# Cross attention on one NeuronCore: scores in row quarters of the array, values in column halves

## The chip, the cores and the metric

The kernel runs on one core of one Trainium2 chip. The metric is the device time of one execution in microseconds (us), as the median of several runs. Beside it stands one execution that the hardware profiler recorded; its trace is what all readings of instructions come from.

## The reference

Two batches of 1024 tokens with 256 features pass four residual blocks in fp32. Only the first is touched by the change: cross attention of the tokens to 77 context rows, with 16 heads of 16 features and a mask on the context rows.

```python
Q = split_heads(query @ Wq.T + bq)     # query: layernorm(x), 2 x 1024 x 256
K = split_heads(key @ Wk.T + bk)       # key, value: the context, 2 x 77 x 256
V = split_heads(value @ Wv.T + bv)
scores = jnp.einsum('bhqd,bhkd->bhqk', Q, K) / scale
scores = jnp.where(mask == 0, -1e10, scores)
attn = jax.nn.softmax(scores, axis=-1)
h = jnp.einsum('bhqk,bhkd->bhqd', attn, V)
return h @ Wo.T + bo
...
x = x + cross_attention(layernorm(x), context)
x = x + self_attention_on_4_of_16_heads(layernorm(x))
x = x + gelu(layernorm(x) @ context.T) @ context      # per batch
x = x + top1_mixture_of_8_experts(layernorm(x))
```

The second block picks four heads per batch from a mean over all tokens, so its weights can be read from memory only when the last tile of that batch has left the first block.

## The kernel before

The 2048 tokens are 16 tiles of 128 (one token a partition). Stage A is the cross attention, one tile after the other, in a software pipeline: `a_step(s)` (L506) issues the scores of tile s, the transposes of the weights of tile s−1, the values of tile s−2, the transpose of the heads' outputs of s−3 and the output projection of s−4. Stage B (self attention, context block and the router) and the experts follow.

**Order.** The whole body stands under a manual schedule for TensorE (PE), VectorE (DVE), ScalarE (ACT) and GpSimd (POOL): each of these engines executes its instructions in the order of the program text. Further work is hung into the steps by a plan: `at("a", s, pos, f, ...)` places f in step s at position pos, and `take` calls what is due. In stage A these are mainly `query` (projection of 512 tokens of the queries, at steps 2, 5, 6, 8 and 9), `do_turn` (transposes of the normalized rows `y_a` and `y_b`, written to `lps`, at steps 1, 3, 4, 5, 7 and, for the second block, 6, 8, 10, 12, 14), `do_rows` (layernorm), and for the second block `route_sums`, `route_mean`, `route_logits`, `route_heads` (step 14: choice of heads and reads of their weights) and `b_qk`. Reads from memory are issued by SyncE, three of them by ScalarE.

**Scores** (`a_scores`, L421). The 256 features are two column groups m of 128, which are 8 heads each. For a column group, a tile's queries stand transposed in `qTa` (features by tokens). The keys stand in `kblk` in block form: for one of HG = 4 heads j a copy of all keys that `hmask` has set to zero outside that head's 16 features and scaled. So a product over 64 partitions, half of the array's rows, gives the scores of 4 heads with 4 × 77 = 308 columns. The two halves gg of the rows write to the two banks of one PSUM tile `sc`. A second product in bf16 (L439) adds −1e10 where the mask is zero: `ones16` times `mneg`, in which three rows of each half hold the three bf16 parts of the number. An fp32 product is two passes, each with a weight load of its own, so one tile has 8 + 4 matmuls.

**Weights of the attention** (`a_weights`, L449). Per column group: DVE takes the maximum per head (`mx`, L453) and subtracts it (`e`, L455), ACT takes the exponential (L459). The two PSUM tiles of a step are the two buffers of the pool `big`.

**Transposes** (`a_transposed`, L461). The 16 × 77 = 1232 weights of a token are cut into 10 chunks of 128; PE transposes them in blocks of 4, 4 and 2 chunks into `pt`, ACT copies each block to `eT` (L469). `pt`, `hps`, `lps` and the other transposes take the two buffers of the pool `trp` (tag `tr`) in turn.

**Values** (`a_values`, L471). Per chunk one product of all 128 tokens with `vblk`: the rows of three heads, masked, and a column of ones for the sum of the weights (3 × 17 = 51 columns), added up in the PSUM tile `av`. After it, in the same function, DVE takes the reciprocal of the sums (`rc`) and normalizes (`hn`). `av`, `po_a`, `qps`, `kps` and others take the two buffers of `accp` (tag `acc`) in turn.

**Start** (L1432 on). In the order of the text: transposes of Wq (`turn_weight`), layernorm of tiles 0 to 3, statistics of tiles 4 to 7 (`do_rows`), transposes of the context (`cps`), of Wk, of the first normalized rows (`do_turn`), key projections `context_k(0)` and `(1)` with the bias `bk_c` and the masked copies to `kblk`, query projections, transposes of Wv, and then the steps. The biases of queries and keys, `bq_c` and `bk_c`, are read as columns by `col_load` (L144): one element for each partition and column group.

## Time and profile before

| | us |
|---|---|
| runs | 623.37, 622.35, 623.32; median 623.32 |
| profiled execution | 623.49 |
| its span, first to last instruction | 621.8 |
| PE busy in the span | 581.7 |
| PE weight loads | 429.3 |
| DVE busy | 359.9 |
| ACT busy | 234.7 |
| POOL busy | 162.0 |
| first scores of tile 0 | at 18.08 |
| first scores of tile 15 | at 121.81 |

Busy times can lie beside each other: the engines work at the same time, and weight loads (PEld) beside the products. Matmuls are pipelined and their ends in the trace are modelled, so the time that a series of them takes is read from one start to the next, not from the sum of durations. In an order in time, each row has the start and length, the engine, the line, the operation, what it writes and reads, the shapes and the number of instructions merged; a bracket tells how long the engine had been idle, and for whom it waited. The granted TensorE clock is 0.978 of full speed in the mean, and full in the first 160 us.

### The profile page before, as it was taken

What the parts mean: (1) busy time and instruction counts of PE and PEld (TensorE: products, weight loads), DVE (VectorE), ACT (ScalarE), POOL (GpSimd) and SP (SyncE); (2) the same over time, 40 slices, a digit from 0 to 9 for tenths busy, and PEclk for the clock granted to TensorE, in tenths of its full rate; (3) what the DMA queues carried; (4) which work ended last, traced back from release to release, by engine and by line L of the source; (5) the groups of instructions that cost most, each with busy time, mean ns of one, the idle gap of its engine ahead of it and who ended that gap; (6) DMA issues with size and microseconds to landing.
All of it is one profiled execution on the core that took longest, in us unless ns stands there. A gap on an engine that the chain in (4) does not pass through costs nothing. (4 is left out here: it accounts for less than half of the span.)

```text
span 621.8 us, 10102 instructions
## 1 busy us (share of the span) xinstructions
PE 581.7 (94%) x3722; PEld 429.3 (69%) x3722; DVE 359.9 (58%) x939; ACT 234.7 (38%) x476; POOL 162.0 (26%) x204
## 2 busy tenths in 40 slices
PE   5999999989999999999999999996797999999994
PEld 4578878866655556656555656564596999999994
DVE  6767667852874356658665767676546433333331
ACT  3555545542655355445445555440021012111110
POOL 6656233222200020403021222200401233333321
PEclk9999999999999999999999999997689899999998
DMA  7100000020001000001000100011993799999940
GB/s 233 34 2 2 1 0 2 1 61 1 1 19 41 1 1 18 17 1 36 1 34 1 35 2 34 2 35 72 353 338 119 255 362 323 360 372 371 344 144 11
DMA packets 49674, 62.75 MB, mean 101 GB/s; under 512 B 11513, under 2 KB 42708, under 8 KB 49622
## 3 DMA queue, kind: packets, MB, share of 16 engines
q1 hardware_dynamic: 46352, 54.04, 25.8%
q0 software_dynamic: 2560, 7.34, 3.2%
q8 instruction: 31, 0.51, 0.3%
q10 hardware_dynamic: 709, 0.68, 0.3%
q14 instruction: 22, 0.17, 0.1%
HBM read 55.76 MB, written 6.82 MB: 101 GB/s over the span
## 5 line engine op out<-in xcount | busy, mean ns | idle before, releaser
L716 DVE TENSOR_REDUCE bnm<-bsc 128x1 f32<-128x1024 f32 x64 | 75.2, 1216 | 14.9 <-PE bsc L702 14.9
L1131 PE MATMUL ph<-ybT,w1s 128*128 128x128 f32 x640 | 79.7, 284 | 3.9 <-DVE ybT L1116 3.9
L1131 PEld LDWEIGHTS ph<-ybT,w1s 128*128 128x128 f32 x640 | 78.4, 200 | 6.0 <-DVE ybT L1116 5.1
L728 PE MATMUL bpt<-ident,be 128*128 128x128 f32 x512 | 73.1, 280 | 3.2 <-DVE v L678 1.2
L1150 PE MATMUL epo<-w2s,ehT 128*128 128x256 f32 x320 | 75.6, 380 | 0.0
L728 PEld LDWEIGHTS bpt<-ident,be 128*128 128x128 f32 x512 | 55.6, 140 | 27.9 <-issue 10.1
L718 ACT ACTIVATE be<-bsc,bnm 128x1024 f32<-128x1024 f32 x64 | 70.8, 1113 | 8.3 <-DVE bnm L716 7.9
L729 DVE COPY beT<-bpt 128x512 f32<-128x512 f32 x64 | 43.9, 686 | 50.4 <-PE bpt L728 50.4
L1138 ACT ACTIVATE ehT<-ph,b1s 128x128 f32<-128x128 f32 x80 | 22.9, 369 | 116.3 <-PE ph L1131 115.1
L702 PE MATMUL bsc<-kT,qT 64*128 64x512 f32 x256 | 64.6, 615 | 0.0
L738 PE MATMUL bov<-beT,v 128*64 128x256 f32 x512 | 63.4, 391 | 0.0
L1150 PEld LDWEIGHTS epo<-w2s,ehT 128*128 128x128 f32 x320 | 57.9, 190 | 6.3
L729 ACT COPY beT<-bpt 128x512 f32<-128x512 f32 x64 | 37.5, 586 | 62.4 <-PE bpt L728 61.4
L1140 DVE TENSOR_SCALAR ehT<-ph,b1s 128x128 f32<-128x128 f32 x80 | 22.5, 343 | 61.2 <-ACT ehT L1138 56.8
L738 PEld LDWEIGHTS bov<-beT,v 128*64 128x64 f32 x512 | 34.4, 139 | 24.6 <-issue 9.4
L1162 POOL DMA_INDIRECT out_dram<-ob,etok x20 | 20.5, 1023 | 94.2 <-DMA out_dram<-ob,etok 40.5
L750 POOL COPY brb<-brc 128x256 f32<-128x256 f32 x16 | 6.4, 398 | 146.5 <-DVE brc L748 146.5
L702 PEld LDWEIGHTS bsc<-kT,qT 64*128 64x128 f32 x256 | 22.5, 186 | 25.1 <-issue 20.7
L477 PE MATMUL av<-vblk,eT 128*128 128x51 f32 x320 | 37.4, 272 | 0.8 <-DVE hn L485 0.8
L477 PEld LDWEIGHTS av<-vblk,eT 128*128 128x128 f32 x320 | 37.1, 192 | 1.6 <-DVE hn L485 1.1
L453 DVE TENSOR_REDUCE mx<-sc 128x8 f32<-128x616 f32 x32 | 25.3, 792 | 16.6 <-PE sc L439 16.6
L469 ACT COPY eT<-pt 128x512 f32<-128x512 f32 (+1 forms) x48 | 23.0, 515 | 25.9 <-PE pt L468 25.1
(253 smaller groups left out, 854.2 us busy)
## 6 DMA issues: line engine op xcount, KB each, us to landing
w1s<-in_L_ffn_w_dram SPq DMA_DIRECT2D x20, 1024.0 KB
w2s<-in_L_ffn_w_dram SPq DMA_DIRECT2D x20, 1024.0 KB
b2s<-in_L_ffn_b_dram SPq DMA_DIRECT2D x20, 128.0 KB
xs<-in_x_dram SPq DMA_DIRECT2D x4, 512.0 KB
ztok<-xs SPq DMA_DIRECT2D x16, 128.0 KB
ztok<-y_d SPq DMA_DIRECT2D x16, 128.0 KB
ws_k<-in_L_ffn_Wk_dram SPq DMA_DIRECT2D x8, 64.0 KB
ws_q<-in_L_ffn_Wq_dram SPq DMA_DIRECT2D x8, 64.0 KB
```

The source lines that it names most:

```text
L453: nc.vector.tensor_reduce(mx, scv, AX.X, ALU.max)
L469: copy(eTs[t][:, c0 : c0 + n, :], pt[:, :n, :])
L477: nc.tensor.matmul(av[:, h0 : h0 + HW, :].rearrange("p h d -> p (h d)"), lhsT=eT[:, c, :], rhs=vblk[:, t // NT, c].rearrange("p h d -> p ( ...
L702: nc.tensor.matmul(sc[h][:, n : n + 512], lhsT=qks[b, "q", m][r, q0 : q0 + P], rhs=qks[b, "k", m][r, n : n + 512], start=True, stop=True,)
L716: nc.vector.tensor_reduce(nm, sc[h], AX.X, ALU.max, negate=True)
L718: nc.scalar.activation(bes[i][:, h], sc[h], AF.Exp, bias=nm, accum_out=sms[g][:, q, s : s + 1])
L728: nc.tensor.transpose(pt[:, k - k0, :], bes[i][:, h, k * P : (k + 1) * P], ident)
L729: copy(beTs[gm][:, h, k0 : k0 + 4, q * P : (q + 1) * P], pt)
L738: nc.tensor.matmul(ovs[gm][h * FD : (h + 1) * FD, :], lhsT=vs[g * TG // NT][:, k, 2 * m + h, :], rhs=beTs[gm][:, h, k, :], start=(k == 0), ...
L1131: nc.tensor.matmul(ph[:, f, :], lhsT=ws[n][0][:, c, f * P : (f + 1) * P], rhs=ybT[:, c, :], start=(c == 0), stop=(c == C - 1),)
L1138: nc.scalar.activation(hT[:, f, :], ph[:, f, :], AF.Relu, bias=b1s[:, f : f + 1])
L1150: nc.tensor.matmul(po, lhsT=hT[:, f, :], rhs=w2s[:, f, :], start=(f == 0), stop=(f == FC - 1))
```

## The change

The scores are computed in G = 4 quarters of the rows, 32 partitions each, with HG = 2 heads and 2 × 77 = 154 columns a product. The four quarters write to four banks, so both `big` buffers of a step are taken at its start, and the two column groups m stand side by side in a bank. To keep the order of the heads, the features of queries and keys are placed in another order: the copies of the transposed Wq and Wk are split in two, one for each ci, with rows in the order (m r x) in place of (r m x). `a_weights` handles 2 × 4 heads per PSUM tile as before.

The values of a chunk are two products of 64 tokens each, in the two halves of the columns, so 40 passes in place of 20. `a_values` now holds only the products and is called right after the scores, before the transposes of tile s−1; reciprocal and normalization became `a_normalized`, after `a_weights` and before the position 1 of the plan.

The biases are read as rows of 32 elements into `brow` and turned by PE in `turn_biases`, which takes a `tr` buffer after the context's transposes and before those of Wk; DVE copies the result to `bcol`. `hmask` and `neg3` are filled for four quarters instead of two halves; `kblk` and `mneg` have two heads a group instead of four.

```diff
-    G = 4
-    HG = H // G
+    HG = 2
+    G = P // (HG * HD)
...
-    def col_load(name, ap):
-        t = acon.tile([P, C], F32, name=name)
-        with nc.allow_non_contiguous_dma(reason="bias columns"):
-            nc.sync.dma_start(t, ap.rearrange("(c p) -> p c", p=P))
-        return t
+    def row_load(i, ap):
+        with nc.allow_non_contiguous_dma(reason="bias rows"):
+            nc.sync.dma_start(
+                brow[i * C : (i + 1) * C].rearrange("m (r x) -> m r x", r=G),
+                ap.rearrange("(r m x) -> m r x", m=C, r=G),
+            )
...
-    for r0 in range(0, P, 64):
-        hm = hmask[r0 : r0 + 64, :]
+    for r0 in range(0, P, P // G):
+        hm = hmask[r0 : r0 + P // G, :]
...
-    for r0 in range(0, P, 64):
+    for r0 in range(0, P, P // G):
         n3 = neg3[r0 : r0 + 3, :]
...
+    bcol = acon.tile([P, 2, C], F32, name="bcol")
+    bk_c, bq_c = bcol[:, 0, :], bcol[:, 1, :]
+
+    def turn_biases():
+        ps = trp.tile([P, 2 * C], F32, name="brps", tag="tr")
+        nc.tensor.transpose(ps, brow, ident[: 2 * C, : 2 * C])
+        nc.vector.tensor_copy(bcol.rearrange("p i c -> p (i c)"), ps)
...
-        nc.scalar.copy(t.rearrange("p c d -> p (c d)"), ps.rearrange("p a b k -> p (a b k)"))
+        if nm in "qk":
+            for ci in range(C):
+                nc.scalar.copy(
+                    t[:, ci].rearrange("p (m r x) -> p r m x", m=C, r=G),
+                    ps[:, ci].rearrange("p b k -> p (b k)").rearrange("p (r m x) -> p r m x", m=C, r=G),
+                )
+        else:
+            nc.scalar.copy(t.rearrange("p c d -> p (c d)"), ps.rearrange("p a b k -> p (a b k)"))
...
+        scs = [
+            big.tile([P, 2, 512], F32, name=f"sc_{t}_{i}", tag="big") for i in range(G // 2)
+        ]
+
+        n = HG * KC
         for m in range(C):
+            outs = [scs[r // 2][:, r % 2, m * n : (m + 1) * n] for r in range(G)]
+            rs = [slice(r * P // G, (r + 1) * P // G) for r in range(G)]
+            for o, r in zip(outs, rs):
                 nc.tensor.matmul(
+                    o, lhsT=qTs[b, "q"][r, m, q0 : q0 + P],
                     rhs=kblk[r, b, m].rearrange("p h k -> p (h k)"),
+                    start=True, stop=False,
                 )
+            for o, r in zip(outs, rs):
                 nc.tensor.matmul(
+                    o, lhsT=ones16[r, :], rhs=mneg[r, b].rearrange("p h k -> p (h k)"),
+                    start=False, stop=True,
                 )
...
+            for q in range(0, P, P // 2):
+                nc.tensor.matmul(
+                    av[q : q + P // 2, h0 : h0 + HW, :].rearrange("p h d -> p (h d)"),
+                    lhsT=eT[:, c, q : q + P // 2],
+                    rhs=vblk[:, t // NT, c].rearrange("p h d -> p (h d)"),
+                    start=(c == 0), stop=(c == NCH - 1), skip_group_check=True,
+                )
+
+    def a_normalized(t):
+        av = avs.pop(t)
...
         scs = a_scores(s) if s < T else None
+        if 0 <= s - 2 < T:
+            a_values(s - 2)
         take("a", s, 0)
...
         if s < T:
             a_weights(s, scs)
+        if 0 <= s - 2 < T:
+            a_normalized(s - 2)
         take("a", s, 1)
-        if 0 <= s - 2 < T:
-            a_values(s - 2)
...
             nc.scalar.copy(ctxT[:, :, b, :], ps)
+        turn_biases()
         turn_weight("k")
```

More of the change, by code (lines that the diff above doesn't have):

```diff
@@ L154 @@
     load_x(4)
-    bk_c = col_load("bk_c", a_bk)
+    brow = acon.tile([2 * C, P], F32, name="brow")
+    row_load(0, a_bk)
     mask_i = acon.tile([P, B, KC], I32, name="mask_i")
@@ L160 @@
     )
-    bq_c = col_load("bq_c", a_bq)
+    row_load(1, a_bq)
     load_raw(nc.sync, "v", a_wv)
@@ L416, in place_v_heads @@
             )
-    es, eTs, hns, hTs = {}, {}, {}, {}
+    es, eTs, avs, hns, hTs = {}, {}, {}, {}, {}
     def a_scores(t):
@@ L423, in a_scores @@
         es[t] = eap.tile([P, H, KC], F32, name=f"e_{t}", tag="e")
-        scs = []
+        scs = [
+            big.tile([P, 2, 512], F32, name=f"sc_{t}_{i}", tag="big") for i in range(G // 2)
+        ]
+        n = HG * KC
         for m in range(C):
-            sc = big.tile([P, 2, 512], F32, name=f"sc_{t}_{m}", tag="big")
-            for gg in range(2):
-                r = slice(gg * 64, gg * 64 + 64)
+            outs = [scs[r // 2][:, r % 2, m * n : (m + 1) * n] for r in range(G)]
+            rs = [slice(r * P // G, (r + 1) * P // G) for r in range(G)]
+            for o, r in zip(outs, rs):
@@ L430, in a_scores @@
                 nc.tensor.matmul(
-                    sc[:, gg, : HG * KC],
-                    lhsT=qTs[b, "q"][r, m, q0 : q0 + P],
+                    o, lhsT=qTs[b, "q"][r, m, q0 : q0 + P],
                     rhs=kblk[r, b, m].rearrange("p h k -> p (h k)"),
-                    start=True,
-                    stop=False,
-                )
-            for gg in range(2):
-                r = slice(gg * 64, gg * 64 + 64)
+                    start=True, stop=False,
+                )
+            for o, r in zip(outs, rs):
@@ L439, in a_scores @@
                 nc.tensor.matmul(
-                    sc[:, gg, : HG * KC],
-                    lhsT=ones16[r, :],
-                    rhs=mneg[r, b].rearrange("p h k -> p (h k)"),
-                    start=False,
-                    stop=True,
+                    o, lhsT=ones16[r, :], rhs=mneg[r, b].rearrange("p h k -> p (h k)"),
+                    start=False, stop=True,
                 )
-            scs.append(sc)
         return scs
     def a_weights(t, scs):
-        for m, sc in enumerate(scs):
-            scv = sc[:, :, : HG * KC].rearrange("p g (h k) -> p g h k", h=HG)
-            mx = small.tile([P, 2, HG], F32, name=f"mx_{t}_{m}", tag="mx", bufs=3)
+        hb = C * HG
@@ L453, in a_weights @@
+        for i, sc in enumerate(scs):
+            scv = sc[:, :, : hb * KC].rearrange("p g (h k) -> p g h k", h=hb)
+            mx = small.tile([P, 2, hb], F32, name=f"mx_{t}_{i}", tag="mx", bufs=3)
             nc.vector.tensor_reduce(mx, scv, AX.X, ALU.max)
-            em = es[t][:, m * 2 * HG : (m + 1) * 2 * HG, :]
+            em = es[t][:, i * 2 * hb : (i + 1) * 2 * hb, :]
             nc.vector.tensor_tensor(
                 em.rearrange("p (g h) k -> p g h k", g=2), scv,
-                mx.unsqueeze(3).to_broadcast([P, 2, HG, KC]), ALU.subtract,
+                mx.unsqueeze(3).to_broadcast([P, 2, hb, KC]), ALU.subtract,
@@ L471, in a_values @@
     def a_values(t):
-        av = accp.tile([P, H, HD + 1], F32, name=f"av_{t}", tag="acc")
+        av = avs[t] = accp.tile([P, H, HD + 1], F32, name=f"av_{t}", tag="acc")
         eT = eTs.pop(t)
@@ L476, in a_values @@
             h0 = head_c[c]
-            nc.tensor.matmul(
-                av[:, h0 : h0 + HW, :].rearrange("p h d -> p (h d)"), lhsT=eT[:, c, :],
-                rhs=vblk[:, t // NT, c].rearrange("p h d -> p (h d)"),
-                start=(c == 0), stop=(c == NCH - 1), skip_group_check=True,
-            )
+            for q in range(0, P, P // 2):
[7 more added lines that the diff above has]
+        av = avs.pop(t)
         rc = small.tile([P, H], F32, name=f"rc_{t}", tag="rc")
```

## The prediction

> **What bounds the kernel now.** I read the windows of the trace first, cut at the starts of the scores of single tiles, then the groups of instructions, then the order in time of one step, of the first 18 us, and the table of waits.
>
> ```profile
> 0.00:18.08 18.08, 11.59 (x40) 7.71 (x41) 11.09 (x53) 6.59 (x11) 12.10 (x41) 1.00 0.72 226
> 18.08:38.22 20.14, 18.90 (x126) 12.93 (x125) 14.16 (x30) 10.98 (x19) 10.92 (x8) 1.00 0.01 4
> 38.22:121.81 83.59, 83.25 (x631) 67.08 (x630) 61.42 (x128) 45.03 (x91) 33.53 (x31) 1.00 0.00 1
> ```
>
> The columns are length, then busy time of TensorE, its weight loads, VectorE, ScalarE and GpSimd. From tile 3 to tile 15 of the cross attention TensorE never rests (83.25 of 83.59 us); VectorE has 27% spare. After the stage TensorE stays the bound to the end (94% of the span), so what this stage gains or loses reaches the end. One step without a query projection (tile 7, 67.11 to 73.56, 6.45 us) in order of time, start and length first:
>
> ```profile
> 67.11 0.79 PE L430 MATMUL sc<-kblk,qTa 64*128 64x308 f32 x4
> 67.73 0.30 PE L439 MATMUL sc<-mneg,ones 64*128 64x308 bf16 x2
> 67.86 0.69 PE L430 MATMUL sc<-kblk,qTa 64*128 64x308 f32 x4
> 68.61 1.09 PE L468 MATMUL pt<-ident,e 128*128 128x128 f32 x8
> 69.36 1.07 ACT L469 COPY eT<-pt 128x512 f32<-128x512 f32 x2 [1.41 <-PE pt L468]
> 69.43 2.31 PEld L477 LDWEIGHTS av<-vblk,eT 128*128 128x128 f32 x20
> 70.32 0.73 ACT L459 ACTIVATE e<-e 128x616 f32<-128x616 f32 x1
> 71.34 0.72 ACT L459 ACTIVATE e<-e 128x616 f32<-128x616 f32 x1 [0.30 <-DVE e L455]
> 71.60 0.27 PEld L468 LDWEIGHTS pt<-ident,e 128*128 128x128 f32 x2
> 72.15 0.37 ACT L469 COPY eT<-pt 128x256 f32<-128x256 f32 x1
> 73.03 0.60 PE L320 MATMUL lps_a<-ident,y_a 128*128 128x128 f32 x4
> ```
>
> The scores hold TensorE for 1.50 us (67.11 to 68.61), the values for 2.17 (69.43 to 71.60). While the values run, ScalarE copies both transposed blocks out, so the third block at 71.60 finds its buffer free. ScalarE's order in a step is two copies, two exponentials, third copy.
>
> Before the first scores:
>
> ```profile
> 8.59 0.72 PEld L348 LDWEIGHTS wps_k<-ident,raw_k 128*128 128x128 f32 x4 [1.50 <-ACT ctxT L1452]
> 9.50 2.00 PE L320 MATMUL lps_a<-ident,y_a 128*128 128x128 f32 x8
> 10.39 0.71 PEld L320 LDWEIGHTS lps_a<-ident,y_a 128*128 128x128 f32 x4 [0.23 <-ACT wkT L351]
> 11.30 2.26 PE L363 MATMUL kps<-ctxT,wkT 128*128 128x154 f32 x8
> 12.38 0.38 DVE L290 TENSOR_SCALAR rs_a<-mv_a 128x2 f32<-128x2 f32 x1
> 12.68 0.23 DVE L1456 TENSOR_SCALAR keep<-mask_i 128x154 f32<-128x154 int32 x1
> ```
>
> Here VectorE runs without a pause to L290, and PE's second `lps_a` waits for the copy of `wkT`: two `tr` buffers in turn.
>
> [...]in the groups, L738 (64 columns) takes 63.4 us for 512 matmuls of 256 elements, 0.124 each, L1150 (all columns) 75.6 for 320, 0.236 each; L728 starts 0.09 us after L738's streaming should be over.[...]139 ns mean at 64 columns (L738), 190 at 128 (L1150).[...]the transposes of `wps_q` at 5.05 take 424 ns, those of `wps_v` at 17.55 272 ns.
>
> **The scores.** Now 0.37 (weights and first pass) + 0.26 + 0.13, then 0.26 + 0.26 + 0.22 with the drain. With two heads a quarter each stream halves, if four run at once: 0.11 weights + 0.13 + 0.13 + 0.11 (the next fp32 weights, longer than the 0.06 of the mask's stream) + 0.13 + 0.13 + 0.06 + 0.09 drain = 0.89.[...] I take **0.95**: 0.55 less. Instructions double, 12 to 24 matmuls, cost unknown; below.
>
> **The values.** Now 20 passes of 0.112, each as long as its 128-column load (2.31 us for 20 loads). With two halves at once a pass is a 64-column load: 0.112 less 0.051 is 0.06; 20 × 0.06 + first load 0.06 + last stream 0.05 + two drains 0.09 is 1.4 to 1.5. I take **1.45**: 0.72 less. Together the transposes of a tile start 2.40 us into its step. Bounds for both: 1.3 us a tile gained, or nothing and more if issue limits (24 + 40 pairs at 0.06, as close as pairs stand anywhere in the groups: 3.8 us, 0.2 worse than 3.67).
>
> **The move of the values.** They now stand ahead of the transposes, so nothing lies between the second block and the third. ScalarE's copy starts 0.75 after the first transpose (69.36 − 68.61) and ends 0.59 later: the third block waits until 1.38 instead of 0.88; `hps` needs the second copy, 1.85 after the start. From there `hps` 0.22, `po` 0.86: free at 2.40 + 2.93 = 5.33. But seven steps of 3 to 14 end in a transpose of y (or small biases) which takes the buffer of the third block, freed behind both exponentials on ScalarE: first copy at 2.40 + 0.75; 0.48 to the second copy and 0.48 to the exponential (two copies take 1.07, one 0.59), 0.73 and 0.80 (one exponential and a small gap each) to the third copy, 0.41 to its end: 6.05; + 0.53 (four transposes) = **6.58**, against 6.45 today, where that chain lay 0.4 under TensorE's own work. So those steps gain nothing. Steps with a query: 5.33 + 1.72 + 0.53 = 7.58 against 8.17. Adding steps 3 to 13, with tile 9's small `hbps` in place of a transpose, tile 11's `b1ps` behind the third block and tile 13's `rps` after `po` (6.58, 6.58, 7.58, 7.58, 6.58, 7.58, 7.20, 6.58, 6.20, 6.58, 5.93) gives 75.0 against 77.1 up to tile 14: 2.1 gained.
>
> VectorE does the same reductions (0.79 and 0.80, twice). Both score buffers now fill together, so its first reduction starts 1.0 after the step instead of 0.96, and the next scores wait for its last subtraction, 4.2 after; hidden under TensorE, except around tile 13, where its 7.4 us (reductions 3.2, normalising 0.75, routing sums, statistics) are later than TensorE and cut the gain to 1.2. In step 14 VectorE's routing block (L575 to L643, 4.5) now follows the normalising instead of preceding it, so the reads of the chosen weights are issued some 0.5 earlier only; but the first `bps_k` waited for `hn` on VectorE (129.83), and that still comes 1.3 earlier. Steps 16 and 17 have two values left: twice 0.72, less the third block's wait of 0.5 and `hps`'s of 0.2 and extra drains, about 0.35. In steps 0 to 2 the second scores wait for both buffers (4.3 after the first instead of 3.4), later repaid by step 2 (8.8 to some 8.0): 0.4. **Sum gained: 0.4 + 1.3 + 0.35 = 2.05.**
>
> **The biases.** 512 four-byte packets become 16; no instruction waited for them for long, so nothing gained. Two weight copies are split in two, 0.1 more on ScalarE. GpSimd does twice the small mask selects (some 1.9 us more before 8 us), under its idle 4.36 us ahead of L291. VectorE saves six small products (1.5 us), but they come after the following. **turn_biases** takes a `tr` buffer between `ctxT` and `wps_k`. In turn, `lps_a` then gets the buffer of the bias transpose, freed by VectorE's small copy, and that stands in VectorE's order behind the statistics of tiles 4 to 7: at 12.7 + 0.2 + 0.1. Behind the waiting `lps_a` on TensorE are the second `lps_a`, `kps`, the queries and the first scores. `lps_a` starts at 13.0 instead of 9.29, saves its 0.2 wait, and the keys come at 14.9 instead of 11.30; half clock applies to both, as now. The queries lose their 0.18 wait for VectorE. First scores at 21.4 instead of 18.08: **3.3 lost**. From 2.9 to 4.6, as idling may leave the queries' first passes at half clock.
>
> **The sum.** The profiled execution took 623.49 (span 621.8 and 1.7 around it), 0.17 over the median of 623.32. 623.49 + 3.3 − 2.05 = 624.74; for the median 624.6.
>
> **Rivals.** (a) *The start is free*: the bias copy is done early, or `lps_a` gets another buffer. Then 623.3 − 2.05 = 621.3, not slower; decided by whether `lps_a` waits for VectorE past 10. For: the wait is only buffer order; against: the 0.23 wait for `wkT` shows that order. (b) *The full packing gain arrives*: the third block's wait and ScalarE's chain prove short, each tile gains 1.27, 16 of them 20, limited by VectorE (61.4 busy in 83.6) to about 16; less 3.3: 610.6. For: TensorE is the bound; against: the copies' order. (c) *Issue limits*: 64 matmuls with their loads at 0.06 make scores and values 3.8 us and start the transposes at 3.9; every step is 1.5 longer than forecast, 14 steps 21: 645; halfway, 634. For: no stretch of the groups shows pairs closer than 0.06 for long; against: L738's and L430's pairs overlap freely.
>
> **Numbers.** Forecast 0.53 (own range 622 to 628), (a) 0.22, (b) 0.08, (c) 0.17. About 0.2%, 1.25 us, is what a measurement here can tell from no change. Faster by more: 0.05 of the forecast's chance, 0.15 of (a), all of (b): 0.28. Within: 0.20 and 0.07: 0.27. Slower: 0.28 and 0.17: 0.45. The range reaches from (a) with ideal packing, 619.5, to halfway into (c), 632; 2 in 10 lie outside.
>
> **What would show it.** Right: `lps_a` at about 13 with a wait for VectorE; quarters of scores overlapping, first transpose 2.3 to 2.5 after the step's start; the third block's load waiting 0.5 for `eT`; steps with y transposes near 6.5, with queries near 7.6. Wrong: `lps_a` near 9.5, steps near 5, or pairs of values 0.1 apart.

## The result, and the profile after

| | before | after |
|---|---|---|
| median of 20 runs each, us | 623.44 | 621.25 |
| lowest and highest | 622.01, 625.19 | 617.19, 625.39 |
| profiled execution; its span | 623.49; 621.8 | 622.26; 620.6 |
| first scores of tile 0 | 18.08 | 20.78 |
| first scores of tile 3, of tile 15 | 38.22, 121.81 | 43.63, 122.83 |
| first `bps_k`, third `bps_k` tile | 129.93, 143.22 | 129.69, 142.34 |

The ratio of after to before is 0.996, 95% interval 0.9943 to 0.9978: 0.4% faster. The forecast was 0.2% slower. The range held the time, the sign was wrong. `bps_k` is the PSUM tile of the second block's key projection, the first work behind stage A.

The windows of the changed kernel, cut at the same places as those of the kernel before (start of the scores of tiles 0, 3 and 15; length, then PE, PEld, DVE, ACT, POOL, granted clock, DMA share, GB/s). The clock in the first row is not a reading, since the trace has no clock record before 17.35 (14.00 in the kernel before):

```profile
0.00:20.78 20.78, 12.02 (x42) 7.97 (x42) 9.80 (x48) 6.71 (x13) 15.22 (x52) 1.00 0.65 199
20.78:43.63 22.85, 20.96 (x181) 15.36 (x180) 14.18 (x30) 10.84 (x19) 9.67 (x8) 0.78 0.01 2
43.63:122.83 79.20, 71.84 (x1016) 53.47 (x1015) 60.53 (x130) 42.64 (x91) 32.99 (x30) 1.00 0.01 2
```

Up to 17.35, and to 14.00 before the change, TensorE runs at half clock: the transposes for Wq follow each other every 0.21 us, those for Wv later every 0.11. So "full in the first 160 us", said above of the kernel before, holds only from 14.00 on, and half clock lasts 3.35 us longer in the changed kernel's start.

Three things differ. The start is 2.7 us longer. Steps 0 to 2 are 2.7 us longer, at a granted clock of 0.78. Steps 3 to 14 are 4.4 us shorter, and TensorE, which rested only 0.3 us there before, now rests 7.4 of 79.2 us. The same tile 7 as before the change, in order of time:

```profile
71.04 0.55 PE L450 MATMUL sc<-kblk,qTa 32*128 32x154 f32 x8
...
71.96 1.37 PE L493 MATMUL av<-vblk,eT 128*64 128x51 f32 x40
...
73.26 1.09 PE L482 MATMUL pt<-ident,e 128*128 128x128 f32 x8
74.01 1.07 ACT L483 COPY eT<-pt 128x512 f32<-128x512 f32 x2 [2.13 <-PE pt L482]
74.65 0.44 PE L482 MATMUL pt<-ident,e 128*128 128x128 f32 x2 [0.29 <-ACT eT L483]
74.97 1.33 ACT L473 ACTIVATE e<-e 128x616 f32<-128x616 f32 x2
75.14 0.20 PEld L513 LDWEIGHTS hps<-ident,hn 128*128 128x128 f32 x2 [0.29 <-ACT eT L483]
76.19 0.37 ACT L483 COPY eT<-pt 128x256 f32<-128x256 f32 x1
76.62 0.66 PE L322 MATMUL lps_a<-ident,y_a 128*128 128x128 f32 x4 [0.18 <-ACT eT L483]
77.20 0.41 PE L450 MATMUL sc<-kblk,qTa 32*128 32x154 f32 x4
```

Scores take 0.92 (71.04 to 71.96; before 1.50), values 1.30 (71.96 to 73.26; before 2.17). The step is 6.16 against 6.45: of 1.45 us saved on TensorE, 0.29 arrive. The rest became waits of TensorE for ScalarE's `eT`: for the third block, for `hps` (the transposes of the heads' outputs), and for the `lps_a` at the end, whose buffer is free only when ScalarE has done two copies, two exponentials and the third copy.

The start of the changed kernel, TensorE's instructions and the bias copy of VectorE:

```profile
9.47 0.18 PEld L348 LDWEIGHTS brps<-ident,brow 4*128 4x128 f32 x1 [1.50 <-ACT ctxT L1474]
11.52 0.72 PEld L322 LDWEIGHTS lps_a<-ident,y_a 128*128 128x128 f32 x4 [1.14 <-ACT wkT L362]
13.31 0.72 PEld L322 LDWEIGHTS lps_a<-ident,y_a 128*128 128x128 f32 x4 [1.08 <-ACT yT_a L323]
13.78 0.15 DVE L349 COPY bcol<-brps 128x4 f32<-128x4 f32 x1
```

The bias copy comes as late as feared (13.78), but no `lps_a` waits for it. They wait for `wkT` and for `yT_a`: the bias transpose holds one of the two `tr` buffers from 9.47 until VectorE's copy at 13.78, and the waits show everything else going through the other, one after the other. That costs less than the 3.3 us that were forecast for waiting on VectorE.

The clock in the early steps, in windows of 2 us (same columns), two of the six that hold it:

```profile
28.00:30.00 2.00, 2.00 (x11) 2.00 (x11) 1.97 (x5) 0.00 (x0) 0.00 (x0) 0.50 0.00 0
...
36.00:38.00 2.00, 2.00 (x40) 2.00 (x40) 1.90 (x3) 0.00 (x0) 0.48 (x1) 0.54 0.00 0
```

And in the order in time, the instruction ahead of it:

```profile
25.14 0.40 PE L450 MATMUL sc<-kblk,qTa 32*128 32x154 f32 x2 [1.00 <-DVE e L469]
```

The quarters of tile 1 need both score buffers of tile 0, and the second is free only after VectorE's last subtraction: TensorE rests 1.00 us. Some 2.5 us later it runs at half clock, for 10.2 us (27.59 to 37.83, by the trace's clock records). Before, the first half of the scores needed one buffer only, and the clock was full there.

### The profile page after: what moved, and what is told of

The parts are those of the page before. It is cut to its first block, busy times and chain, and to the rows that moved or that the text cites. A ratio compares the mean times of both kernels' runs of the same rounds, so it can differ in the third digit from the quotient of the medians.

```text
span 620.6 us, 11135 instructions
## 1 busy us (share of the span) xinstructions
PE 571.1 (92%) x4235; PEld 416.4 (67%) x4235; DVE 357.1 (58%) x934; ACT 232.3 (37%) x478; POOL 163.1 (26%) x214
## 3 DMA queue, kind: packets, MB, share of 16 engines
q0 software_dynamic: 2560, 7.34, 3.3%
## 5 line engine op out<-in xcount | busy, mean ns | idle before, releaser
L1172 PE MATMUL epo<-w2s,ehT 128*128 128x256 f32 x320 | 77.6, 387 | 0.0
L1172 PEld LDWEIGHTS epo<-w2s,ehT 128*128 128x128 f32 x320 | 59.3, 195 | 6.9
L724 PEld LDWEIGHTS bsc<-kT,qT 64*128 64x128 f32 x256 | 22.5, 186 | 25.1 <-issue 20.7
L482 PE MATMUL pt<-ident,e 128*128 128x128 f32 x160 | 25.4, 293 | 4.4 <-ACT eT L483 4.4
L1124 POOL DMA_INDIRECT zb<-ztok,etok x20 | 19.7, 986 | 27.5 <-issue 14.2
```

The source lines that it names most:

```text
L482: nc.tensor.transpose(pt[:, c - c0, :], e[:, off_c[c] : off_c[c] + P], ident)
L724: nc.tensor.matmul(sc[h][:, n : n + 512], lhsT=qks[b, "q", m][r, q0 : q0 + P], rhs=qks[b, "k", m][r, n : n + 512], start=True, stop=True,)
L1172: nc.tensor.matmul(po, lhsT=hT[:, f, :], rhs=w2s[:, f, :], start=(f == 0), stop=(f == FC - 1))
```

## The experiments

Theory A: the packing gains what it should, the new order of the steps gives most of it back through ScalarE, and the start and the half clock cost the rest. Rival B, in the form that each run needs: the gain is lost elsewhere (VectorE, TensorE's issue, the packing itself). Each kernel ran beside the kernel before on the same chip; the medians of the latter were 623.90 (for the first four kernels below), 623.07 (next four), 623.24 (next three), 623.56 (next), and 623.58 (last three). Medians of different groups are therefore comparable only to some 0.8 us; the ratios are not affected. "Late turn" and "twelve transposes" below are the edits of the first two.

**The late turn of the biases.** Changed kernel, one call moved:

```diff
-        turn_biases()
         turn_weight("k")
         do_turn("a", 0)
         do_turn("a", 2)
+        turn_biases()
```

> The biases are turned after the first four transposes of normalized rows instead of before those of Wk; all else as in the changed kernel. Theory A (the start lost to the buffer order): both blocks of lps_a follow each other without waiting for ScalarE's copies, the first scores of tile 0 come 1.5 to 2 us earlier than in the changed kernel when set against the landing of raw_q, and the median falls by 1.5 to 3 (to 618 to 620). Theory B (the start is bound by the landing of the weights and by VectorE's statistics): the first scores move by less than 0.5 and the median stays within 1 of 621.25.

Measured: 620.64 (615.35 to 621.01, 7 runs), ratio 0.9927 (0.9899 to 0.9956). First scores at 18.74, 2.04 earlier than in the changed kernel with Wq's transposes equally late (5.89 and 5.87), and the two blocks of `lps_a` follow each other without a wait: A. So the place of the turn costs 2.0 us in these two executions: 1.6 up to the key projections (12.59 against 14.22), 0.4 after them, where the clock is full from 12.72 on here and from 17.35 in the changed kernel. The rest of the change is not free at the start: Wq's transposes begin at 5.44 to 5.99 in the ten traces of kernels that read the biases as rows, at 5.02 to 5.27 in the seven that read them as columns. No run separates which of the edits at the start does that.

The median is over A's range, and 0.6 from the changed kernel's: the time alone would speak for B. The runs fall apart: 615.4 twice, at a mean clock of 0.975, 617.4 once, at 0.972, and near 620.8 four times, at 0.970. The profiled one was of the first kind:

```profile
18.74:38.00 19.26, 16.79 (x182) 11.90 (x181) 14.18 (x30) 10.75 (x19) 10.73 (x8) 1.00 0.01 2
```

With full clock steps 0 to 2 take 19.26, against 22.85 in the changed kernel: the half clock cost 3.6 us there. From tile 3 to 15 the two kernels take the same 79.20.

**Twelve transposes.** Changed kernel; in step 0 TensorE transposes the identity twelve times into a spare buffer that nothing reads:

```diff
+    def warm():
+        ps = trp.tile([P, 4, P], F32, name="warmps", tag="tr")
+        for i in range(12):
+            nc.tensor.transpose(ps[:, i % 4, :], ident, ident)
...
+    at("a", 0, 0, warm)
```

> The changed kernel with twelve more transposes of the identity, read by nobody, after the context's values of step 0, where TensorE otherwise idles 1.0 us before the scores of tile 1. Theory A (half clock in the start comes from idling there): the clock between 20 and 40 us is full in the profile, the mean clocks of the runs are at or over 0.975, and the median falls to 617 to 619. Theory B (the quarters and halves themselves lower the clock, or the idling of 10 to 14 us does): clock and median as in the changed kernel, 0.97 and 621.

Measured: 617.45 (616.98 to 618.15, 4 runs), ratio 0.9894 (0.9872 to 0.9917): 3.8 under the changed kernel's median, though TensorE does more. The clock is full in the early steps, and the spread is 1.2 us in these 4 runs (mean clock 0.975 to 0.981), 8.2 in the 20 of the changed kernel (0.965 to 0.981):

```profile
21.57:40.84 19.27, 17.79 (x193) 13.18 (x192) 14.18 (x30) 10.75 (x19) 8.09 (x7) 1.00 0.01 2
```

With work in the place of the rest, the profiled execution has no half clock from 21.57 to 120.05. The start has the early turn of the changed kernel, and the first scores come at 21.57 here against 20.78 there; the clock is full from 18.88 on here.

**Values between the second and third block again** (normalizing stays early):

```diff
         scs = a_scores(s) if s < T else None
-        if 0 <= s - 2 < T:
-            a_values(s - 2)
         take("a", s, 0)
...
             a_transposed(s - 1, 4, nc.scalar.copy)
+        if 0 <= s - 2 < T:
+            a_values(s - 2)
```

> The changed kernel with the values moved back between the second and third block of transposes. Theory A (two waits for ScalarE's copies cost 0.5 and 0.2 a tile since the move, and ScalarE's chain starts later): the third block waits no more, steps with a transpose of y shorten from 6.2 to 5.8 to 6.0, those with a query from 7.48 to 6.8 to 7.0, and the median falls by 3 to 5. Theory B (the move pays because the normalising leaves VectorE earlier, and VectorE is the limit): steps keep their lengths or grow, median 621 to 623.

Measured: 618.63 (618.38 to 619.58, 5 runs), ratio 0.9921 (0.9902 to 0.994). Steps with a transpose of y take 5.90 to 5.97 instead of 6.16 to 6.26: A; those with a query fall only from 7.48 to between 7.34 and 7.42, less than A had. The profiled execution had a half clock too, of 3.4 us around 126, with a rest of 2.2 us before the first `bps_k` (125.1).

**Only the values' halves.** The kernel before, with `a_values`' products in two halves of the columns, in the old place; nothing else of the change:

```diff
-            nc.tensor.matmul(
-                av[:, h0 : h0 + HW, :].rearrange("p h d -> p (h d)"), lhsT=eT[:, c, :],
...
+            for q in range(0, P, P // 2):
+                nc.tensor.matmul(
+                    av[q : q + P // 2, h0 : h0 + HW, :].rearrange("p h d -> p (h d)"),
+                    lhsT=eT[:, c, q : q + P // 2],
...
```

> The kernel before with nothing but the values in two column halves, in their old place. Theory A: values take 1.3 to 1.4 instead of 2.17, steps with a transpose of y go from 6.45 to about 6.0 (then bound by ScalarE's third copy), those with a query from 8.17 to 7.4; start as before; median 615.5 to 618.5. Theory B (the gain of the changed kernel needs the quarters): less than 2 us gained, 621.5 or more.

Measured: 614.06 (613.58 to 617.29, 5 runs), ratio 0.9853 (0.9827 to 0.9878). One part of the change alone brings more than four times the whole change's gain (9.8 against 2.2 us), more than A had, too. Its step of tile 7 is 5.85.

**Late turn and twelve transposes together**: both diffs above, on the changed kernel.

> The changed kernel with two edits: the turn of the biases stands after the transposes of the normalized rows, and twelve transposes of the identity, which nothing reads, keep TensorE busy in step 0. Theory A (the loss at the start and the half clock of the early steps are two separate costs): first scores at about 18.7 us as in the late turn alone, tile 3 at about 38.0, the granted clock full through the first 100 us, and all runs within 1.5 us of each other: median 615.0 to 616.0, 5 us under the late turn alone. Theory B (the half clock does not come from the idling before the scores of tile 1): runs spread from 615 to 621 as with the late turn alone, median 618 or more.

Measured: 615.23 (614.84 to 616.46, 5 runs), ratio 0.9875 (0.9854 to 0.9896). The two costs add: 6.0 us under the changed kernel. A's full clock through 100 us was not right: the profiled execution has 3.4 us of half clock at 44, behind a rest of 1.1 us in step 3.

**Third block first.** As the last, with

```diff
             a_transposed(s - 1, 4, nc.scalar.copy)
+            a_transposed(s - 1, 8, nc.scalar.copy)
+            del es[s - 1]
         if s < T:
             a_weights(s, scs)
...
-        if 0 <= s - 1 < T:
-            a_transposed(s - 1, 8, nc.scalar.copy)
-            del es[s - 1]
```

> As the kernel with the late turn and the twelve transposes, and the third block of transposes with its copy put ahead of both exponentials on ScalarE. Theory A (ScalarE's order holds the steps at 6.2 us): steps of 3 to 12 with a transpose of y fall from 6.2 to about 5.7, with a query from 7.48 to about 7.1, tile 14 starts 3.5 to 5 us earlier after tile 3, and the whole is 2 to 4 us shorter than without the edit: 611 to 613.5. Theory B (VectorE sets the end of the stage): tile 14 starts earlier, but the first key projection of the second block stays within 1 us of where it was, and the time with it: 614.5 or more.

Measured: 613.91 (612.16 to 614.38, 5 runs), ratio 0.9846 (0.9824 to 0.9867). Steps with a transpose of y fall to 5.76 to 5.80 (tile 3's to 5.15), as A says; those with a query stay at 7.48 to 7.62, which A had wrong. Tile 3 to 14 takes 70.1 instead of the changed kernel's 73.0. The median is only 1.3 under the kernel without the edit, with overlapping intervals: it is the steps that show A, not the time.

**Both packings in the old order** (late turn, twelve transposes; values between the blocks, normalizing behind position 1):

```diff
         scs = a_scores(s) if s < T else None
-        if 0 <= s - 2 < T:
-            a_values(s - 2)
...
             a_transposed(s - 1, 4, nc.scalar.copy)
+        if 0 <= s - 2 < T:
+            a_values(s - 2)
         if s < T:
             a_weights(s, scs)
+        take("a", s, 1)
         if 0 <= s - 2 < T:
             a_normalized(s - 2)
-        take("a", s, 1)
```

> As the kernel with the late turn and the twelve transposes, but with values and normalizing where the kernel before has them (values between second and third block, normalizing behind the plan's position 1): both packings in the old order. Theory A (quarters and halves each keep their gain when the order is the old one): steps with a transpose of y near 5.9 or below, since the scores take 0.58 less than in the halves alone; 611 to 613, under the 614.1 of the halves alone. Theory B (once the values are in halves, ScalarE and VectorE hold the steps, and faster scores only make longer waits): steps of 5.85 to 6.0 as with the halves alone, 613.5 to 615.

Measured: 615.31 (613.35 to 616.41, 5 runs), ratio 0.9871 (0.9848 to 0.9895), steps of 5.90 to 5.96: B. With the values in halves, the quarters bring nothing in the old order. The order in time of tile 7 shows why; it begins at 64.34 with the halves alone, whose lines come first, and at 64.29 here:

```profile
65.30 0.80 DVE L453 TENSOR_REDUCE mx<-sc 128x8 f32<-128x616 f32 x1 [2.58 <-PE sc L439]
...
68.57 0.72 ACT L459 ACTIVATE e<-e 128x616 f32<-128x616 f32 x1 [0.30 <-DVE e L455]
69.19 0.35 ACT L469 COPY eT<-pt 128x256 f32<-128x256 f32 x1
```

```profile
65.30 0.80 DVE L467 TENSOR_REDUCE mx<-sc 128x8 f32<-128x616 f32 x1 [3.13 <-PE sc L456]
...
68.58 0.72 ACT L473 ACTIVATE e<-e 128x616 f32<-128x616 f32 x1 [0.82 <-DVE e L469]
69.20 0.35 ACT L483 COPY eT<-pt 128x256 f32<-128x256 f32 x1
```

VectorE's first maximum starts 0.96 after the step's start with halves, where it needs only the first column group's scores, and 1.01 with quarters, where all scores end together. Its two maxima and two subtractions take 3.3, then come the second exponential, the third copy and the transposes. This chain is as long as the step, with either packing. (With halves alone TensorE's own work is almost as long, as the run with the copy between shows below.)

**Only the quarters**, in the same old order with the same two edits; values whole:

```diff
-            for q in range(0, P, P // 2):
+            for q in range(0, P, P):
                 nc.tensor.matmul(
-                    av[q : q + P // 2, h0 : h0 + HW, :].rearrange("p h d -> p (h d)"),
-                    lhsT=eT[:, c, q : q + P // 2],
+                    av[q : q + P, h0 : h0 + HW, :].rearrange("p h d -> p (h d)"),
+                    lhsT=eT[:, c, q : q + P],
```

> The same old order, late turn and twelve transposes, with the scores in quarters and the values whole (128 tokens a product). Theory A (the quarters are worth 0.58 a tile where TensorE is the bound): steps with a transpose of y at 5.9 to 6.0 against 6.45 before, tile 14 some 5 to 6 us earlier after tile 3, 617 to 619.5. Theory B (the quarters' gain is lost in waits in this order too): steps near 6.4, 621 to 624.

Measured: 618.67 (617.06 to 619.60, 6 runs), ratio 0.9918 (0.9898 to 0.9938), steps of 5.90 to 5.96: A. Alone the quarters are worth having, as TensorE was the bound until the same chain of 5.9 took over. The profiled execution has 3.4 us of half clock from 122.7, behind a rest of 1.5 us.

**Normalizing early, halves only.** The kernel with the values' halves, `a_normalized` split off as in the change, and

```diff
-        take("a", s, 1)
         if 0 <= s - 2 < T:
             a_values(s - 2)
+            a_normalized(s - 2)
+        take("a", s, 1)
```

> The kernel before with the values in halves of the columns, in the old place on TensorE, and the normalizing ahead of the plan's position 1 on VectorE, as the changed kernel has it. Theory A (the normalizing behind the choice of heads holds TensorE at tiles 14 and 15): the wait of the values for VectorE at tile 15 (0.92 us with the halves alone) is gone, the first key projection of the second block comes 6.9 us after tile 15 instead of 8.2, and the time is 612.5 to 613.3 against 614.1. Theory B (VectorE has the same work to do and the projection comes when it is done): the projection stays within 0.3 us of 124.0 and the time at 613.7 to 614.5.

Measured: 612.75 (611.96 to 615.07, 5 runs), ratio 0.984 (0.9821 to 0.9859). `bps_k` waits for `hn` on VectorE in both, in the halves alone (first lines) as here (second):

```profile
119.31 1.38 PE L478 MATMUL av<-vblk,eT 128*64 128x51 f32 x40 [0.92 <-DVE hn L487]
123.99 1.96 PE L655 MATMUL bps_k<-yT_b,ws_k 128*128 128x512 f32 x4 [1.85 <-DVE hn L487]
```

```profile
122.15 1.95 PE L660 MATMUL bps_k<-yT_b,ws_k 128*128 128x512 f32 x4 [1.62 <-DVE hn L491]
```

The wait of the values at tile 15 is gone and the projection is 1.8 earlier, 7.0 after tile 15 instead of 8.2. Moving the normalizing is the part of the new order that helps. In the medians the step is 1.3 us, of which 0.7 is the difference of the kernel before in the two groups; the intervals of the two ratios overlap, so the time alone does not settle it.

**Third copy between the exponentials, halves only** (`a_weights` now takes which of the two exponentials it is to do):

```diff
         if s < T:
-            a_weights(s, scs)
-        take("a", s, 1)
+            a_weights(s, scs, 0)
         if 0 <= s - 2 < T:
             a_values(s - 2)
         if 0 <= s - 1 < T:
             a_transposed(s - 1, 8, nc.scalar.copy)
             del es[s - 1]
+        if s < T:
+            a_weights(s, scs, 1)
+        take("a", s, 1)
+        if 0 <= s - 2 < T:
+            a_normalized(s - 2)
```

> The kernel before with the values in halves, and ScalarE's copy of the third block put between the two exponentials instead of behind both; TensorE's and VectorE's orders are the old ones. Theory A (the chain scores, VectorE's two reductions and subtractions, second exponential, third copy, transposes of y holds a step at 5.85): steps with a transpose of y fall to 5.4 to 5.6, tile 14 some 2.5 to 4 us earlier, 611 to 612.5. Theory B (TensorE's own work is the bound there, 5.85 busy of 5.85): steps stay at 5.85 and the time at 613.5 to 614.5.

Measured: 614.01 (612.70 to 614.51, 5 runs), ratio 0.9846 (0.9831 to 0.9861). Steps fall only from 5.85 to 5.72, because there TensorE is busy throughout (5.71 of 5.71 us in tile 7): B. Tile 15 comes 2.6 and `bps_k` 2.2 earlier, but the span is only 0.7 shorter: the rest of the program took 1.5 longer. Behind the third `bps_k` tile, where no kernel here changes anything, the profiled executions take between 475.7 and 478.9 us. These two stay within 0.25 us of each other for the first 290 us of that, and part where both have stretches of half clock, at different places. Half clock is not more here: the mean between 380 and 500 us is 0.90, with halves alone 0.89. Why the 1.5 us are lost stays open.

**Both packings, third copy between the exponentials, normalizing early** (late turn, twelve transposes). The step now reads, behind the first two blocks:

```python
if s < T:
    a_weights(s, scs, 0)
if 0 <= s - 2 < T:
    a_values(s - 2)
if 0 <= s - 1 < T:
    a_transposed(s - 1, 8, nc.scalar.copy)
    del es[s - 1]
if s < T:
    a_weights(s, scs, 1)
if 0 <= s - 2 < T:
    a_normalized(s - 2)
take("a", s, 1)
```

> Both packings with the late turn of the biases and the twelve transposes, values between the second and the third block of transposes, the third copy between the exponentials, normalizing ahead of the plan's position 1. Theory A (with the chain over ScalarE cut, TensorE is the bound again and the quarters show): steps with a transpose of y 5.2 to 5.4, with a query 6.9 to 7.1, tile 14 at 105 us, 609 to 611. Theory B (what the quarters free turns into other waits, on the score buffers and VectorE): steps of 5.7 or more, 612 to 614.

Measured: 610.12 (609.23 to 610.40, 5 runs), ratio 0.9788 (0.9775 to 0.9801): the fastest of all, 11 us under the changed kernel. Tile 7, from 62.14 to 67.27, takes 5.13:

```profile
64.88 0.72 ACT L473 ACTIVATE e<-e 128x616 f32<-128x616 f32 x1
65.85 0.37 ACT L483 COPY eT<-pt 128x256 f32<-128x256 f32 x1 [0.25 <-PE pt L482]
66.42 0.72 ACT L473 ACTIVATE e<-e 128x616 f32<-128x616 f32 x1 [0.20 <-DVE e L469]
66.74 0.60 PE L322 MATMUL lps_a<-ident,y_a 128*128 128x128 f32 x4
```

ScalarE's waiting time between the exponentials holds the copy, the values cover the copies of the first two blocks, and TensorE is busy for the whole step. Here, and only here, the quarters' gain shows in full beside that of the halves (5.71 with halves alone, 0.58 more). That holds for the steps with a transpose of y; those with a query take 7.34 to 8.19, more than A's 6.9 to 7.1, and TensorE rests in them again (1.10 us at 73.13). The profiled execution also has 6.8 us of half clock from 117.0, in a rest of 2.6 us (115.6 to 118.2) before the first `bps_k`; from that to the second it takes 8.59, where the halves alone take 5.86.

**A rest in the kernel before.** The first maximum of tile 0 taken three times:

```diff
-            nc.vector.tensor_reduce(mx, scv, AX.X, ALU.max)
+            for _ in range(3 if (t, m) == (0, 0) else 1):
+                nc.vector.tensor_reduce(mx, scv, AX.X, ALU.max)
```

> The kernel before with one thing added: the first maximum of tile 0 is taken three times, 1.6 us more on VectorE, so that TensorE rests about 1.5 us before the scores of tile 1. Theory A (a rest of a microsecond or more lets TensorE fall to half clock in part of the executions): the executions without it take 1.2 to 1.7 us more than the kernel before, those with it 3 to 6.5 us more, at a mean clock some 0.003 to 0.008 lower; spread over 3 us. Theory B (the half clock belongs to the packed products, not to the rest): all runs 1.2 to 1.7 us above the kernel before, with a spread and a mean clock like its own, and full clock through the first 100 us of the profile.

Measured: 625.26 (623.50 to 627.17, 22 runs), ratio 1.0024 (1.0012 to 1.0036), mean clock 0.975 to 0.978 in all, as in the kernel before (0.970 in one of its 27 runs): no half clock beyond that kernel's own, and none in the early steps of the profile: B. Theory A, in the form that any such rest brings it, failed; the rest was 0.95 and then 0.62 us, shorter than meant:

```profile
22.71 0.79 PE L430 MATMUL sc<-kblk,qTa 64*128 64x308 f32 x4 [0.95 <-DVE e L456]
```

**A longer rest in it:**

```diff
-            nc.vector.tensor_reduce(mx, scv, AX.X, ALU.max)
+            for _ in range(5 if (t, m) == (0, 0) else 1):
+                nc.vector.tensor_reduce(mx, scv, AX.X, ALU.max)
```

> The kernel before with the first maximum of tile 0 taken five times, 3.2 us more on VectorE, so that TensorE rests about 2.5 us before the scores of tile 1. Theory C (the half clock needs a rest and the products of quarter height around it): no half clock in the early steps, 3.2 to 3.5 us over the kernel before, spread as its own. Theory D (the length of the rest alone decides): half clock in most executions, 6 to 9 us over the kernel before, mean clock 0.965 to 0.972.

Measured: 630.20 (626.51 to 631.88, 6 runs), ratio 1.0098 (1.0072 to 1.0124). Two runs at 626.5 and 626.8 with a clock of 0.978, four at 630.1 to 631.9 with 0.970. The profiled one, of the first kind, shows the rest:

```profile
24.39 0.79 PE L430 MATMUL sc<-kblk,qTa 64*128 64x308 f32 x4 [2.62 <-DVE e L456]
```

The trace is not of a slower one, so where their half clock lies is not shown. But 0.978 against 0.970 is an estimated 10 us at half clock, none of the 43 runs of the kernel before beside it is under 0.975, and the 3.7 us are those of the changed kernel's half clock (3.6). So, by the mean clocks, a rest of 2.62 us brings half clock without any packing: D.

**A longer rest in the changed kernel** (late turn):

```diff
-            nc.vector.tensor_reduce(mx, scv, AX.X, ALU.max)
+            for _ in range(3 if (t, i) == (0, 0) else 1):
+                nc.vector.tensor_reduce(mx, scv, AX.X, ALU.max)
```

> The changed kernel with the late turn of the biases, and the first maximum of tile 0 taken three times, so that TensorE rests 2.5 us instead of 1.0 before the scores of tile 1. If a rest among quarter products brings the half clock (C, and D as well), nearly all executions have it: median 621 to 624, mean clock 0.970 and below. If neither, 616.5 to 617.5, which is 1.6 us over the undisturbed executions of the late turn alone (615.4).

Measured: 622.24 (618.19 to 624.41, 22 runs), ratio 0.9967 (0.9951 to 0.9982). Seventeen of 22 runs have a clock of 0.973 or less, where "nearly all" was expected; the profiled one, after rests of 1.59 and 1.01 us, has half clock from 26.7 to 40.3. A rest of the same two parts as with three maxima in the kernel before, longer by 0.6 and 0.4, and now it comes in most executions. With the late turn alone and its rest of 1.0 us it was five of 7, so more often is not shown; longer is: seven runs have 0.967 here, none there.

**Halves only, in the new order.** Scores in halves of the rows, values in halves of the columns and early, normalizing as in the changed kernel. Beside the halves alone:

```diff
         scs = a_scores(s) if s < T else None
+        if 0 <= s - 2 < T:
+            a_values(s - 2)
         take("a", s, 0)
...
             a_weights(s, scs)
-        take("a", s, 1)
         if 0 <= s - 2 < T:
-            a_values(s - 2)
+            a_normalized(s - 2)
+        take("a", s, 1)
```

> The kernel before with the values in halves and the changed kernel's order (values right after the scores, normalizing ahead of position 1); scores in halves of the rows, biases as before. Theory A (in this order a step is the scores, the values and then the chain over ScalarE, so that faster scores shorten it one for one): steps with a transpose of y 6.7 to 6.85, with a query 8.0 to 8.1, 620.5 to 623. Theory B (the chain starts at the maxima on VectorE, which do not wait for the values): steps near 6.3, 615 to 617.5. In both no half clock in the early steps under C.

Measured: 623.66 (620.79 to 625.70, 22 runs), ratio 0.9996 (0.9985 to 1.0007). Steps with a transpose of y take 6.75 to 6.81, with a query 8.07 to 8.37: A, and 0.7 us over its range in the median. The same packing that gains 9.8 us in the old order gains nothing in the new one. Tile 7, which starts at 67.92:

```profile
69.42 1.38 PE L478 MATMUL av<-vblk,eT 128*64 128x51 f32 x40
...
72.43 1.34 ACT L459 ACTIVATE e<-e 128x616 f32<-128x616 f32 x2
73.66 0.37 ACT L469 COPY eT<-pt 128x256 f32<-128x256 f32 x1
```

From the values' start to the next scores it is the chain of the changed kernel, here 5.25 (69.42 to 74.67), there 5.24 (71.96 to 77.20). Ahead of it stand the scores, 1.50 here, 0.92 there.

Packing and order together, medians in us (those with quarters have the late turn and the twelve transposes; the kernel before had 623.07 to 623.90 beside them):

| | old order | new order | third copy between |
|---|---|---|---|
| scores and values as before | 623.4 | not run | not run |
| values in halves | 614.06 | 623.66 | 614.01 |
| scores in quarters | 618.67 | not run | not run |
| both | 615.31 | 615.23 | 610.12 |

The third column's last kernel also has the normalizing early.

## Why the prediction was wrong

Two terms of the sum were mis-sized and one was missing. The gain was set at 2.05 and came to some 7.1 at full clock: 4.4 instead of 1.3 from tile 3 to 15, 1.9 instead of 0.35 behind it, 0.9 instead of 0.4 ahead of it. The start was set at 3.3 and cost 2.7. The half clock behind the new rest in the early steps had no term, and took 3.6 back. The chain and the longer start were real. What turned the sign is the price of the chain over ScalarE: the five full steps with a transpose of y (tiles 3, 4, 7, 10 and 12) are together 1.8 shorter than forecast, and with that alone put right the sum is a gain of 0.6; with only the start put right it stays a loss of 0.65.

- **Scores and values, right.** 0.95 and 1.45 forecast, 0.92 and 1.30 measured; the first transpose stands 2.22 into the step instead of 2.40. What the prediction calls a drain is in the traces 0.09 more between starts where the shape changes: 0.22 from the mask's products to the transposes of the kernel before, 0.13 from the mask's products to scores of the same shape; 0.15 from the values to the transposes of the changed kernel, 0.06 from one pass of the values to the next. What TensorE does in it is not shown. The rival of issue limits (c) is out: 40 passes with their loads take 1.30 us, 0.033 each, half of the 0.06 that I had taken for the closest.
- **The chain over ScalarE, right in kind, too long.** "those steps gain nothing" at 6.58 was the step that failed in the sum of the stage (75.0 to tile 14, 73.0 measured): they take 6.16 to 6.26. In tile 7, 0.18 of the 0.42 comes from scores and values, and 0.31 from the exponentials: 1.53 forecast from the first one's start to the third copy, 1.22 measured (74.97 to 76.19), since back to back the pair takes 1.33 and there is no small gap; the end is 0.07 longer. Tiles 3 to 13 gained 4.2 instead of 2.1. The halves alone in the new order show the chain: with scores 0.58 longer, the step is 0.59 longer.
- **VectorE's cut at tile 13, not as thought.** Tile 13 takes 6.60 against 5.93 in my list, as the routing waits for `ym` (0.65), but the other steps keep their gain, so the 0.9 for it was not to be taken off. The prediction first says that this cuts the gain to 1.2; its sum then has 1.3.
- **Tile 15 on.** I gave 0.35 to steps 16 and 17 and counted the earlier `hn` as nothing apart. From tile 15 to `bps_k` it is 6.87 instead of 8.11, 1.2 gained, and 0.64 more to the third `bps_k` tile. The run with only the normalizing moved shows that the 1.2 is the order on VectorE (6.97 instead of 8.19 there); the 0.64 it does not have, and they stay unexplained.
- **The start, wrong in mechanism.** "In turn, `lps_a` then gets the buffer of the bias transpose" failed: `lps_a` got the other buffer and waited for ScalarE's copies instead. The loss is 2.0 (changed kernel against the late turn) instead of 3.3, and up to 2.9 in the two other traces with the early turn (first scores at 21.57 and 21.66), where the half clock of the start ends later still, at 18.88 and 19.17. That risk was named, as a range of 2.9 to 4.6; in the changed kernel's trace the first pass of the queries takes 0.85 (16.27 to 17.13), each from 17.67 on 0.43. Rival (a)'s "another buffer" is what happened, though not for nothing; that its 621.3 is the measured time is luck, since its start of no cost, its gain of 2.05 and its missing half clock are all wrong. And "nothing gained" for the bias reads left out that Wq comes later with them.
- **Steps 0 to 2: the new wait was seen, its price was not.** I had "the second scores wait for both buffers" and a gain of 0.4. At full clock it is 0.9; but the rest of 1.0 us brings a half clock in many executions (14 of the 20 have a mean clock of 0.973 or less), 3.6 us in the profiled one, 3.8 in the median (twelve transposes). I had bounded idling for the queries of the start only.

From the profiled executions, up to the third `bps_k` tile: start +2.7 (0.8 of it Wq's later arrival), steps 0 to 2 −0.9 and +3.6 for the clock, tiles 3 to 14 −4.4, tile 15 to `bps_k` −1.2, then −0.64: −0.9, as measured (142.34 against 143.22). Forecast was +3.3 − 2.05. Rival (b), the whole packing gain, was the right picture of what the packing can do, but it takes another order: 610.1 with that order, 610.6 named. The nearness is luck in part: the 610.6 holds a loss of 3.3 at the start, which that kernel, with the late turn, does not have.

**The half clock.** It followed a rest of 1.0 us of TensorE in the changed kernel in a part of the executions, and so it did, by the mean clocks, one of 2.6 us in the kernel before. In the traces of these two kernels, all starts and ends of half clock lie on one grid of 3.413 us, to 1.3 ns, from the first clock record to the experts (the last one's end apart, where the record stops). The 10.2 us here are three steps of it, those after the longer rest four, those in the kernel with both packings and the copy between two, those at 44, 122.7 and 126 one. The grid lies differently in each execution: counted from the start of the span, its points are 0.3 us behind the multiples of 3.413 in the changed kernel, and 1.0, 2.1, 2.8, 3.2 and 3.4 in five others (estimates, from the first start of half clock in each). That this is why one kernel has half clock in some executions and not in others is a guess. One step at half clock lowers the mean clock of a run by an estimated 0.0027 (half of 3.413 in 621), so that 0.978 against 0.970 is three steps. Shown is that the spread goes when the rest is filled (615.35 to 621.01 becomes 614.84 to 616.46), and that a longer rest alone came with 0.970 in four of 6 runs. Not settled is why 1.0 us is enough with quarters and 0.95 plus 0.62 us was not with halves. TensorE's busy share does not tell: the step of the grid ahead of the half clock (24.18 to 27.59) was busy for 0.72 in the changed kernel, while in the kernel before with the longer rest, wherever the grid lies, one step was busy for 0.53 or less (from windows of 0.5 us), and full clock followed. Whether the products of quarter height, or their shorter total time around the rest, make the difference, no run separates.

## What to carry to other kernels

When the bound engine gets faster, price the chain of the others before the gain: here the halves alone were worth 9.8 us, nothing once they stood ahead of the transposes, and beside the halves the quarters only paid after one copy was put between two exponentials. Move one thing at a time, the order and the packing apart. And when a change makes TensorE wait for about a microsecond among short work, look at the granted clock and the spread of the runs: here a wait of 1.00 us cost 3.6 us more in the profiled execution.

## What was not expected of the hardware

- A rest of 1.00 us (24.1 to 25.1) was followed by 10 us at half clock; another execution of nearly the same stretch, with a rest of 1.0 us, was at full clock from 18.74 to 38.00 (late turn).
- Products of 64 columns with their loads follow each other at 0.033 us in the mean over 40.
- Two exponentials of 128 × 616 take 0.72 each alone and 1.33 as a pair.
- A transpose of 4 rows kept a buffer for 4.3 us (9.47 to 13.78) because its copy stood late in VectorE's order; the weight loads of the two blocks of `lps_a` then each waited 1.1 us for the one left.
